# A two-layer decoder in float32: layer-1 self-attention in two steps a unit instead of three, with other PSUM banks, copies and context transposes

## The chip, the cores and the metric

The kernel runs on one core of a Trainium2 chip. TensorE (PE) multiplies and transposes, VectorE (DVE), ScalarE (ACT) and GpSimd (POOL) do the rest, and SyncE (SP) and POOL issue DMAs. PE writes to PSUM[...]. The metric is the device time of one execution in microseconds, the median of several.

## The reference, cut to what matters

A batch of 8 sequences of 512 tokens, width 256, in float32, goes through two layers. The normalisation is without weights.

```python
x = layernorm(x + L0_attn(x))            # 16 heads of 16, scores times a decay
x = layernorm(x + L0_xattn(x, ctx, ctx)) # 64 context tokens, masked
x = layernorm(x + L0_ffn(x))             # butterfly transforms
x = layernorm(x + L1_attn(x))            # below
x = layernorm(x + L1_xattn(x, ctx))      # below
x = layernorm(x + L1_ffn(x))             # 8 experts, the best 2 for each token

# L1_attn: 16 heads of 64, rotary positions, causal
q, latent = x @ wq.T, x @ w_kv_down.T
k, v = latent @ w_k_up.T, latent @ w_v_up.T
q, k = q * cos + rotate_half(q) * sin, k * cos + rotate_half(k) * sin
attn = softmax(q @ k.T / 8 + causal);  out = (attn @ v) @ wo.T

# L1_xattn: 8 heads of 64; keys and values of x (512) and of ctx (64) side by side
k, v = concat(x @ Wk1, ctx @ Wk2), concat(x @ Wv1, ctx @ Wv2)
out = softmax(x @ Wq1 @ k.T / 8) @ v @ Wo + bo
```

## The kernel before, in words

All eight sequences stay in SBUF. The stages follow one another: layer-0 self-attention (with the butterfly matrices built on POOL beside it), layer-0 context attention and feed-forward, layer-1 self-attention, layer-1 context attention with the routing of tokens, experts. The program is written as a sequence of operations. A list scheduler gives each engine its order from costs and dependencies, except where `manual_schedule(engines={PE})` keeps PE in the order of the program: that holds for the context stage of layer 1, not for its self-attention. `_pipeline` (L32) runs units through stages with offsets, and after each step it takes one piece from a list of put-off work (`put_off`: halves of the output projection).

PSUM is split into three pools: `s_tile` for scores (two banks a tile), `t_tile` for transposes and `o_tile` for sums. In layer 1 they hold 2, 2 and 2 tiles. `evac` (L98) copies PSUM to SBUF, in turn on DVE (L102) and ACT (L104).

**Layer-0 self-attention.** A unit is a sequence and four heads; `l0_project` (three units ahead) makes q and k and copies them with ACT (L404, L405). `l0_maxima` (L419, L424) makes scores for the row maxima, `l0_probs` (L468 to L477) the transposed probabilities, `l0_values` (L488) the sums. `later` holds the previous sequence's projection and the next one's preparation; `normed` then runs on ACT (L215).

**Layer-1 self-attention.** A unit is a pair of heads (b, c), with 8 units in a sequence and 64 in all. `l1_prepare` gives `share` once a sequence (x transposed, latent), `q_and_k` (s_q L844 and L845; the rope multiplies L849 and L850 on DVE; then four DMAs L853 from POOL that add the half turned by 32 rows into qk) and `v` (t_v L860, copied by ACT L862). `l1_pre` takes these from `ahead`. Rows of scores go in the groups (0, 1), (2,), (3,), that is 128 and 256, 384, and 512 columns; each group is a step. The stages of a step are, one behind the other: `l1_scores` (L899, then `masked_softmax`: L265 adds the mask and reduces on DVE, L275 scales the maximum, L277 is ACT's exp; then `scaled`: L883, L885 on DVE), `nothing`, `l1_transposes` (L931, copies by `evac`), `l1_values` (L955). The output projection `o_out` is L233.

**Layer-1 context attention.** A unit is a sequence and a pair of heads, with four row blocks (steps). `l1x_pre` makes q, k and v (L1020, L1027), and once a sequence the context values (o_v2, in the profile o_v L1008, 64 rows); `l1x_scores` 512 and 64 columns for each head (L1047, L1048), the maximum on DVE (L1049), the exp on ACT (L1050); `l1x_transposes` the four 128-column blocks of each head (L287); `l1x_last_transposes` the last 64 columns (L1069, one for each head, into half of the partitions); `l1x_values` the sums (L1081, and L1088 for the context).

Zero fills of a scratch area for the routing (64 DMAs from SP) run at the start of layer 1.

Of the kernel before, what the change touches and what calls it, by code (L numbers as in the profile page):

```python
# [49 lines left out]
def decoder_kernel(ctx: ExitStack, tc: tile.TileContext, a: dict, out: bass.AP):  # L50
# [19 lines left out]
    @contextmanager  # L70
    def psum(name, s, t, o):

        with (
            tc.tile_pool(name=f"ps_s{name}", bufs=s, space=PSUM) as pp["s"],
            tc.tile_pool(name=f"ps_t{name}", bufs=t, space=PSUM) as pp["t"],
            tc.tile_pool(name=f"ps_o{name}", bufs=o, space=PSUM) as pp["o"],
        ):
            yield
# [14 lines left out]
    def o_tile(name):  # L93
        return pp["o"].tile([P, 512], F32, tag="o", name=name)

# [128 lines left out]
    def project_and_norm(b, lhs, w, n, plus, later=None):  # L224
# [3 lines left out]
        def piece(i2):  # L228
            o = o_tile("o_out").rearrange("p (i n) -> p i n", i=2)
# [23 lines left out]
    def pt_tile():  # L253
        return ph.tile([P, 2, NT, P], F32, tag="pt", name="pt")
# [4 lines left out]
    def masked_softmax(s, p, m, n, scale, add_or_mult, sums, at):  # L259

        mx = col("mx", 2)
        nm = col("nm", 2)
        op, reduced = add_or_mult
        for j in range(2):
            dve.tensor_tensor_reduce(  # L265
                out=p[:, j, 0:n],
                in0=s[:, j, 0:n],
                in1=m,
                scale=1.0,
                scalar=-3.0e38,  # L270
                op0=op,
                op1=reduced,
                accum_out=mx[:, j : j + 1],
            )
        dve.tensor_scalar(nm, mx, -scale, None, ALU.mult)  # L275
        for j in range(2):
            act.activation(  # L277
                p[:, j, 0:n], p[:, j, 0:n], AF.Exp,
                bias=nm[:, j : j + 1], scale=scale, accum_out=sums[:, at + j : at + j + 1],
            )  # L280
# [262 lines left out]
    with tc.tile_pool(name="bfly", bufs=1, side="right") as bfly, phase("l0_self") as ph, psum("a", 3, 1, 1):  # L543
# [36 lines left out]
        for n, (b, g) in enumerate(units):  # L580
# [3 lines left out]
            for kt in range(NT):  # L584
# [17 lines left out]
                elif later:  # L602
                    later.pop(0)()
                for _ in range(3 - kt % 2):
                    next(butterfly, None)
            if n + 3 < len(units):
                l0_project(*units[n + 3])
# [12 lines left out]
    ctx.enter_context(psum("b", 2, 2, 2))  # L620
# [205 lines left out]

    def l1_prepare(b, c):
# [3 lines left out]
        def share():  # L831
            xT = x_transposed(b)
            latT = work.tile([P, S], F32, tag="lat", name="lat")
            o = o_tile("o_lat")
# [37 lines left out]
    def l1_pre(b, c, m):  # L872

        if (b, c, m) == (0, 0, 0):
            for _ in range(3):
                ahead.pop(0)()
        if ahead and (m or c == 7):
            ahead.pop(0)()
# [8 lines left out]
    put_off = []  # L887

    def l1_scores(b, c, m):
# [18 lines left out]
        for g, i in enumerate(GROUPS[m]):  # L908
            n = (i + 1) * P
            masked_softmax(  # L910
                s[:, :, at : at + n], p[:, :, at : at + n], causal[:, S - n : S], n, 1.0 / 8.0, (ALU.add, ALU.max), sums, 2 * g
# [12 lines left out]
    def l1_transposes(b, c, m):  # L924
        p = live.pop(("p", b, c, m))
        pt = pt_tile()
        order = [at for block in l1_blocks(m) for _, at in block]
        for j in range(2):
# [3 lines left out]
            evac(pt[:, j, 0 : len(order), :], t[:, 0 : len(order), :])  # L932
# [33 lines left out]
    with phase("l1_self") as ph:  # L966
        _pipeline(
            [(b, c, m) for b in range(NB) for c in range(8) for m in range(len(GROUPS))],
            [l1_pre, l1_scores, nothing, l1_transposes, l1_values],
            put_off,  # L970
        )
# [17 lines left out]
    for c in range(4):  # L989
        o = o_tile("o_k2")  # L990
# [10 lines left out]
    def l1x_pre(b, c, i):  # L1001
        if i:
            return
        if c == 0:
            xT = x_transposed(b)
            o = o_tile("o_v2")
            for kc in range(KC):
                pe.matmul(  # L1008
                    o[0:S2, :], lhsT=ctxT[:, kc, b * S2 : (b + 1) * S2], rhs=wv2[:, kc, :], start=(kc == 0), stop=(kc == KC - 1)
                )  # L1010
            vx = work.tile([P, S], F32, tag="lat", name="vx")
            evac(vx[0:S2, :], o[0:S2, :])
            live["xT", b], live["vx", b] = xT, vx
# [24 lines left out]
    def l1x_scores(b, c, i):  # L1038
# [4 lines left out]
        for j in range(2):  # L1043
# [12 lines left out]
    def l1x_transposes(b, c, i):  # L1056
        p = live["p", b, c, i]
        if i == 0:
            live["pt", b, c] = pts[c % 2], ph.tile([P, 2, S], F32, tag="pt2", name="pt2")
        pt, _ = live["pt", b, c]  # L1060
        probs_transposed(p, [pt[j][:, :, i * P : (i + 1) * P] for j in range(2)], NT)

    def l1x_last_transposes(b, c, i):

        p = live.pop(("p", b, c, i))
        _, pt2 = live["pt", b, c]
        t = t_tile("tP2")
        for j in range(2):
            pe.transpose(t[0:S2, j, :], p[:, j, S : S + S2], ident)  # L1069
        evac(pt2[0:S2, :, i * P : (i + 1) * P], t[0:S2, 0:2, :])  # L1070

    def l1x_values(b, c, k):
# [83 lines left out]
    def route_picks(b):  # L1156
        xnT = live.pop(("xnT", b))
        o = o_tile("o_r")[:, 0 : NT * NE].rearrange("p (i e) -> p i e", e=NE)
# [36 lines left out]
    def route_places(b):  # L1195

        picks, both = live.pop(("picks", b))
        o = o_tile("o_rank")
# [184 lines left out]
    def moe_down(n):  # L1383
# [3 lines left out]
        o = o_tile("o_y").rearrange("p (i n) -> p i n", i=TILES)  # L1387
# [162 lines left out]
```

## Time and profile before

| | |
|---|---|
| median of 3 runs | 3716.97 us (3712.23 to 3719.49) |
| profiled execution | 3704.71 us, span 3703.0 us |
| granted clock of PE, mean | 0.961 |
| busy: PE, DVE, ACT, POOL | 3483.6, 2190.3, 1447.7, 1091.5 us |
| layer-1 self-attention | from 1266 to 2226 us |
| layer-1 context attention | from 2226 to 3135 us |
| experts | from 3135 us on |

The times of lines and waits below are of the one profiled execution, which is 12.3 us under the median. A row of the page's fifth section or of the groups view names line, engine, operation, tiles, shapes and count; then the busy time in us and the mean of one in ns; then the engine's idle time just before, and what ended it. In the view of waits a row is: what waited, what it waited for, and the total in us, the number of times and the longest. In the timeline a row begins with the start and the length in us.

### The profile page before, as it was taken

How to read it: one execution, taken by the hardware profiler on the slowest of the kernel's cores; microseconds unless marked ns; L12 is line 12 of the kernel's file. 1: busy time of each engine (PE TensorE's matmuls, PEld its weight loads, DVE VectorE, ACT ScalarE, POOL GpSimd, SP SyncE). 2: the span in 40 equal slices, each digit the busy share in tenths (PEclk: the TensorE clock that was granted, in tenths of full speed). 3: DMA queues.
4: the chain of work that ended last, by engine and by line, in shares of the span. 5: the costliest groups of instructions: out<-in, count | busy, mean ns of one | idle time of the engine just before them, and what ended most of it. 6: DMA issues, size and time to landing. Idle time of an engine off the chain costs nothing. (4 is left out here: it accounts for less than half of the span.)

```text
span 3703.0 us, 53042 instructions
## 1 busy us (share of the span) xinstructions
PE 3483.6 (94%) x19862; PEld 2149.2 (58%) x19862; DVE 2190.3 (59%) x6160; ACT 1447.7 (39%) x2949; POOL 1091.5 (29%) x960
## 2 busy tenths in 40 slices
PE   8999899988999899999999999999999998999995
PEld 3344334446666556665666665555555555888884
DVE  5766777647666377778777775665666655110102
ACT  2444444443333244445444443433334333222222
POOL 3877787751211122222222210010101101222222
PEclk8999999987999999999999999999999999999997
DMA  4100011120000395233222320000000001766674
GB/s 130 30 24 24 24 37 36 35 59 9 4 1 1 84 277 120 35 41 40 37 35 35 41 41 1 6 13 18 18 11 14 18 12 58 241 188 180 185 232 136
DMA packets 165363, 233.94 MB, mean 63 GB/s; under 512 B 26441, under 2 KB 128521, under 8 KB 165106
## 3 DMA queue, kind: packets, MB, share of 16 engines
q1 hardware_dynamic: 138370, 174.78, 15.1%
q0 software_dynamic: 25584, 51.57, 9.4%
q10 hardware_dynamic: 1152, 4.19, 0.3%
q8 instruction: 157, 2.57, 0.3%
q14 instruction: 100, 0.82, 0.1%
HBM read 135.83 MB, written 61.11 MB: 53 GB/s over the span
## 5 line engine op out<-in xcount | busy, mean ns | idle before, releaser
L424 DVE CUSTOM_DVE_ANT_0 scored<-s_sc,decay 128x512 f32<-128x512 f32 x512 | 323.2, 687 | 231.1 <-PE s_sc L419 229.9
L853 POOL DMA_DIRECT2D qk<-turned x256 | 202.8, 1206 | 668.8 <-PE t_v L860 284.1
L477 ACT ACTIVATE pt<-s_st 128x1024 f32<-128x1024 f32 x256 | 261.3, 1024 | 263.0 <-PE s_st L473 232.0
L277 ACT ACTIVATE p<-p,nm 128x128 f32<-128x128 f32 (+3 forms) x512 | 283.1, 554 | 160.4 <-DVE nm L275 157.5
L104 ACT COPY pt<-tP 128x512 f32<-128x512 f32 (+2 forms) x416 | 212.5, 511 | 298.3 <-PE tP L931 196.9
L1050 ACT ACTIVATE p<-s_sc,nm 128x576 f32<-128x576 f32 x256 | 189.7, 743 | 294.6 <-DVE nm L1049 256.5
L885 DVE TENSOR_SCALAR p<-p,rsum 128x576 f32<-128x576 f32 (+4 forms) x768 | 296.2, 427 | 5.5
L1410 DVE TENSOR_SCALAR y<-o_y,share 128x256 f32<-128x256 f32 x71 | 31.4, 480 | 403.6 <-PE o_y L1390 403.6
L1373 PE MATMUL s_h<-xnT,we 128*128 128x256 f32 (+1 forms) x1248 | 262.4, 364 | 1.9 <-DMA we<-in_mo_w 1.9
L102 DVE COPY pt<-tP 128x512 f32<-128x512 f32 (+2 forms) x416 | 248.3, 597 | 14.8 <-PE tP L1069 6.8
L1390 PE MATMUL o_y<-we,h 128*128 128x256 f32 x1136 | 251.6, 379 | 0.0
L265 DVE CUSTOM_DVE_ANT_0 p<-s_sc,tabs 128x128 f32<-128x128 f32 (+3 forms) x512 | 233.0, 484 | 20.7 <-PE s_sc L899 20.7
L1373 PEld LDWEIGHTS s_h<-xnT,we 128*128 128x128 f32 x1248 | 218.1, 193 | 27.1 <-DMA we<-in_mo_w 2.3
L1390 PEld LDWEIGHTS o_y<-we,h 128*128 128x128 f32 x1136 | 215.2, 190 | 28.9
L1411 POOL DMA_INDIRECT total<-y,to x71 | 110.1, 1551 | 397.3 <-DVE y L1410 206.0
L899 PE MATMUL s_sc<-qk 64*128 64x256 f32 (+3 forms) x1024 | 207.8, 477 | 18.3 <-DMA qk<-turned 16.3
L1049 DVE TENSOR_REDUCE nm<-s_sc 128x1 f32<-128x576 f32 x256 | 183.2, 749 | 57.2 <-PE s_sc L1048 56.7
L931 PEld LDWEIGHTS tP<-ident,p 128*128 128x128 f32 x1280 | 137.6, 141 | 127.2 <-issue 59.9
L931 PE MATMUL tP<-ident,p 128*128 128x128 f32 x1280 | 193.9, 284 | 12.0 <-DVE pt L102 8.0
L419 PE MATMUL s_sc<-k,q 32*128 32x512 f32 x1024 | 174.4, 680 | 28.4 <-ACT k L405 26.1
L1216 POOL DMA_INDIRECT rows_in<-z,irow x64 | 63.0, 985 | 451.9 <-DVE hit L1211 349.6
L955 PE MATMUL o_pv<-pt,vc 128*64 128x128 f32 (+1 forms) x2304 | 185.5, 294 | 0.0
(282 smaller groups left out, 6657.1 us busy)
## 6 DMA issues: line engine op xcount, KB each, us to landing
we<-in_mo_w SPq DMA_DIRECT2D x78, 1024.0 KB, 6.1
rows_in<-zero SPq DMA_DIRECT2D x64, 530.0 KB, 11.4
qk<-turned POOLq DMA_DIRECT2D x256, 128.0 KB, 4.5
coef<-in_ff_upw SPq DMA_DIRECT2D x40, 256.0 KB, 3.3
coef<-in_ff_dnw SPq DMA_DIRECT2D x40, 256.0 KB, 3.3
xr<-rows_in SPq DMA_DIRECT2D x32, 265.0 KB, 6.3
x<-in_x SPq DMA_DIRECT2D x8, 512.0 KB, 9.7
total<-x SPq DMA_DIRECT2D x8, 512.0 KB, 2.9
```

The lines of the kernel that those rows point to most:

```text
L102: dve.tensor_copy(dst, src)
L104: act.copy(dst, src)
L265: dve.tensor_tensor_reduce(out=p[:, j, 0:n], in0=s[:, j, 0:n], in1=m, scale=1.0, scalar=-3.0e38, op0=op, op1=reduced, accum_out=mx[:, j : ...
L277: act.activation(p[:, j, 0:n], p[:, j, 0:n], AF.Exp, bias=nm[:, j : j + 1], scale=scale, accum_out=sums[:, at + j : at + j + 1],)
L424: dve.tensor_tensor_reduce(out=scored[:, h, :], in0=s[:, j, :], in1=decay[:, i, :], scale=1.0, scalar=-3.0e38, op0=ALU.mult, op1=ALU.max, ...
L477: act.activation(pt, s, AF.Exp, scale=1.0 / 16.0)
L853: pool.dma_start(out=qk[h : h + 32], in_=other[g : g + 32], accum_op=ALU.add)
L885: dve.tensor_scalar(p[:, j, 0:n], p[:, j, 0:n], rsum[:, j : j + 1], None, ALU.mult)
L899: pe.matmul(s[:, j, at : at + n], lhsT=q[h : h + 64, i * P : (i + 1) * P], rhs=k[h : h + 64, 0:n], start=True, stop=True,)
L931: pe.transpose(t[:, n, :], p[:, j, at * P : (at + 1) * P], ident)
L1373: pe.matmul(s[:, j, :], lhsT=w1[:, c, f * P : (f + 1) * P], rhs=xnT[:, c, :], start=(c == 0), stop=(c == KC - 1),)
L1390: pe.matmul(o[:, i, :], lhsT=h[:, f, i * P : (i + 1) * P], rhs=w2[:, f, :], start=(f == 0), stop=(f == 7),)
```

## The change

- In layer 0 `l0_project` of the unit three ahead stands before the piece from `later` in the last step of a unit.
- The PSUM pools are made with `reuse_waits="tile"`. From layer-1 self-attention on they hold 2 score tiles, 3 for transposes and 1 for sums; o_out, o_lat, o_v2, o_k2, o_r, o_rank and o_y take a tile for transposes (`u_tile`).
- `masked_softmax` reduces the negated, scaled scores, so that the operation L275 is gone.
- Layer-1 self-attention has two steps a unit, the row groups (0, 1) and then (2, 3). The stages `nothing` and one step of delay are gone; a step issues scores, transposes of the previous step's first group, the preparing piece, transposes of its second group, and values of the step before that. The copies of transposes are all on ACT, into three buffers. As before, PE's order in this stage comes from the list.
- In the context stage the last 64 columns of the two heads lie side by side (the second head's scores put the context first), and one full transpose takes both, ahead of the other transposes of the step. Context values are made for two sequences at once; two small DMAs turn their halves into a second copy, so that each head finds its rows in its own half of the partitions.

The lines left out exchange `o_tile` for `u_tile` only.

```diff
+        pool_of = partial(tc.tile_pool, space=PSUM, reuse_waits="tile")
         with (
-            tc.tile_pool(name=f"ps_s{name}", bufs=s, space=PSUM) as pp["s"],
-            tc.tile_pool(name=f"ps_t{name}", bufs=t, space=PSUM) as pp["t"],
-            tc.tile_pool(name=f"ps_o{name}", bufs=o, space=PSUM) as pp["o"],
+            pool_of(name=f"ps_s{name}", bufs=s) as pp["s"],
+            pool_of(name=f"ps_t{name}", bufs=t) as pp["t"],
+            pool_of(name=f"ps_o{name}", bufs=o) as pp["o"],
         ):
+            pp["one"] = o == 1
             yield
...
         return pp["o"].tile([P, 512], F32, tag="o", name=name)
+    def u_tile(name):
+        return t_tile(name).rearrange("p i n -> p (i n)") if pp["one"] else o_tile(name)
...
         def piece(i2):
-            o = o_tile("o_out").rearrange("p (i n) -> p i n", i=2)
+            o = u_tile("o_out").rearrange("p (i n) -> p i n", i=2)
             for j in range(2):
...
-    def pt_tile():
-        return ph.tile([P, 2, NT, P], F32, tag="pt", name="pt")
+    def pt_tile(bufs=2):
+        return ph.tile([P, 2, NT, P], F32, tag="pt", name="pt", bufs=bufs)
...
-    def masked_softmax(s, p, m, n, scale, add_or_mult, sums, at):
-        mx = col("mx", 2)
+    def masked_softmax(s, p, m, n, scale, sums, at):
         nm = col("nm", 2)
-        op, reduced = add_or_mult
         for j in range(2):
             dve.tensor_tensor_reduce(
...
                 in1=m,
-                scale=1.0,
-                scalar=-3.0e38,
-                op0=op,
-                op1=reduced,
-                accum_out=mx[:, j : j + 1],
+                scale=-scale,
+                scalar=3.0e38,
+                op0=ALU.add,
+                op1=ALU.min,
+                accum_out=nm[:, j : j + 1],
             )
-        dve.tensor_scalar(nm, mx, -scale, None, ALU.mult)
         for j in range(2):
...
                 p[:, j, 0:n], p[:, j, 0:n], AF.Exp,
-                bias=nm[:, j : j + 1], scale=scale, accum_out=sums[:, at + j : at + j + 1],
+                bias=nm[:, j : j + 1], scale=-1.0, accum_out=sums[:, at + j : at + j + 1],
             )
...
                             later.extend(l0_output(b - 1))
-                elif later:
-                    later.pop(0)()
+                else:
+                    if kt and n + 3 < len(units):
+                        l0_project(*units[n + 3])
+                    if later:
+                        later.pop(0)()
                 for _ in range(3 - kt % 2):
                     next(butterfly, None)
-            if n + 3 < len(units):
-                l0_project(*units[n + 3])
         l0_values(*units[-1], NT - 1)
...
-    ctx.enter_context(psum("b", 2, 2, 2))
+    banks = ExitStack()
+    banks.enter_context(psum("b", 2, 2, 2))
...
+    banks.close()
+    ctx.enter_context(psum("c", 2, 3, 1))
     def l1_prepare(b, c):
...
-    def l1_pre(b, c, m):
-        if (b, c, m) == (0, 0, 0):
-            for _ in range(3):
+    STEPS = ((0,), (1, 2))
+    def l1_pre(b, c, step):
+        for _ in range(2 if (c, step) == (6, 1) else 1):
+            if ahead:
                 ahead.pop(0)()
-        if ahead and (m or c == 7):
-            ahead.pop(0)()
...
     put_off = []
+    def groups(stage, some=slice(None)):
+        def run(b, c, step):
+            for m in STEPS[step][some]:
+                stage(b, c, m)
+        return run
...
             masked_softmax(
-                s[:, :, at : at + n], p[:, :, at : at + n], causal[:, S - n : S], n, 1.0 / 8.0, (ALU.add, ALU.max), sums, 2 * g
+                s[:, :, at : at + n], p[:, :, at : at + n], causal[:, S - n : S], n, 1.0 / 8.0, sums, 2 * g
             )
...
         p = live.pop(("p", b, c, m))
-        pt = pt_tile()
+        pt = pt_tile(bufs=3)
         order = [at for block in l1_blocks(m) for _, at in block]
...
                 pe.transpose(t[:, n, :], p[:, j, at * P : (at + 1) * P], ident)
-            evac(pt[:, j, 0 : len(order), :], t[:, 0 : len(order), :])
+            act.copy(pt[:, j, 0 : len(order), :], t[:, 0 : len(order), :])
         live["pt", b, c, m] = pt
...
     with phase("l1_self") as ph:
+        for _ in range(3):
+            ahead.pop(0)()
         _pipeline(
-            [(b, c, m) for b in range(NB) for c in range(8) for m in range(len(GROUPS))],
-            [l1_pre, l1_scores, nothing, l1_transposes, l1_values],
+            [(b, c, step) for b in range(NB) for c in range(8) for step in range(len(STEPS))],
+            [
+                (0, groups(l1_scores)),
+                (1, groups(l1_transposes, slice(0, 1))),
+                (0, l1_pre),
+                (1, groups(l1_transposes, slice(1, 2))),
+                (2, groups(l1_values)),
+            ],
             put_off,
...
             xT = x_transposed(b)
-            o = o_tile("o_v2")
-            for kc in range(KC):
-                pe.matmul(
-                    o[0:S2, :], lhsT=ctxT[:, kc, b * S2 : (b + 1) * S2], rhs=wv2[:, kc, :], start=(kc == 0), stop=(kc == KC - 1)
-                )
-            vx = work.tile([P, S], F32, tag="lat", name="vx")
-            evac(vx[0:S2, :], o[0:S2, :])
-            live["xT", b], live["vx", b] = xT, vx
+            if b % 2 == 0:
+                o = u_tile("o_v2")
+                for kc in range(KC):
+                    pe.matmul(
+                        o, lhsT=ctxT[:, kc, b * S2 : (b + 2) * S2], rhs=wv2[:, kc, :], start=(kc == 0), stop=(kc == KC - 1)
+                    )
+                vx = [ph.tile([P, S], F32, tag=f"vx{n}", name="vx") for n in range(2)]
+                evac(vx[0], o)
+                for n in range(2):
+                    sp.dma_start(out=vx[1][S2 * n : S2 * (n + 1)], in_=vx[0][S2 * (1 - n) : S2 * (2 - n)])
+                live["vx", b], live["vx", b + 1] = vx, vx[::-1]
+            live["xT", b] = xT
         xT = live["xT", b]
...
             s = s_tile("s_sc").rearrange("p t n -> p (t n)")
-            pe.matmul(s[:, 0:S], lhsT=lhsT, rhs=k[h : h + 64, :], start=True, stop=True)
-            pe.matmul(s[:, S : S + S2], lhsT=lhsT, rhs=k2[h : h + 64, c, b * S2 : (b + 1) * S2], start=True, stop=True)
-            dve.tensor_reduce(nm[:, j : j + 1], s[:, 0 : S + S2], AX.X, ALU.max, negate=True)
-            act.activation(
-                p[:, j, :], s[:, 0 : S + S2], AF.Exp, bias=nm[:, j : j + 1], accum_out=sums[:, j : j + 1]
-            )
+            pe.matmul(s[:, S * j : S * (j + 1)], lhsT=lhsT, rhs=k[h : h + 64, :], start=True, stop=True)
+            at = S - S2 * j
+            pe.matmul(s[:, at : at + S2], lhsT=lhsT, rhs=k2[h : h + 64, c, b * S2 : (b + 1) * S2], start=True, stop=True)
+            s = s[:, at * j : at * j + S + S2]
+            dve.tensor_reduce(nm[:, j : j + 1], s, AX.X, ALU.max, negate=True)
+            act.activation(p[:, j, :], s, AF.Exp, bias=nm[:, j : j + 1], accum_out=sums[:, j : j + 1])
         scaled(p, sums, S + S2)
...
     def l1x_transposes(b, c, i):
-        p = live["p", b, c, i]
+        p = live.pop(("p", b, c, i)).rearrange("p j n -> p (j n)")
         if i == 0:
-            live["pt", b, c] = pts[c % 2], ph.tile([P, 2, S], F32, tag="pt2", name="pt2")
-        pt, _ = live["pt", b, c]
-        probs_transposed(p, [pt[j][:, :, i * P : (i + 1) * P] for j in range(2)], NT)
-    def l1x_last_transposes(b, c, i):
-        p = live.pop(("p", b, c, i))
-        _, pt2 = live["pt", b, c]
-        t = t_tile("tP2")
+            live["pt", b, c] = pts[c % 2], ph.tile([P, S], F32, tag="pt2", name="pt2")
+        pt, pt2 = live["pt", b, c]
+        t = t_tile("tP2")[:, 0, :]
+        pe.transpose(t, p[:, S : S + P], ident)
+        evac(pt2[:, i * P : (i + 1) * P], t)
         for j in range(2):
-            pe.transpose(t[0:S2, j, :], p[:, j, S : S + S2], ident)
-        evac(pt2[0:S2, :, i * P : (i + 1) * P], t[0:S2, 0:2, :])
+            t = t_tile("tP")
+            for k in range(NT):
+                pe.transpose(t[:, k, :], p[:, (S + P) * j + k * P : (S + P) * j + (k + 1) * P], ident)
+            evac(pt[j][:, :, i * P : (i + 1) * P], t)
...
             h = c * P + 64 * j
-            pe.matmul(o[64 * j : 64 * (j + 1)], lhsT=vx[0:S2, h : h + 64], rhs=pt2[0:S2, j, :], start=False, stop=True)
+            pe.matmul(o[64 * j : 64 * (j + 1)], lhsT=vx[j][64 * j : 64 * (j + 1), h : h + 64], rhs=pt2[64 * j : 64 * (j + 1), :], start=False, stop=True)
...
             [(b, c, i) for b in range(NB) for c in range(4) for i in range(NT)],
-            [(0, l1x_pre), (1, l1x_scores), (3, l1x_transposes), (7, l1x_values), (3, l1x_last_transposes)],
+            [(0, l1x_pre), (1, l1x_scores), (3, l1x_transposes), (7, l1x_values)],
             put_off,
```

More of the change, by code (lines that the diff above doesn't have):

```diff
@@ L833, in share @@
             latT = work.tile([P, S], F32, tag="lat", name="lat")
-            o = o_tile("o_lat")
+            o = u_tile("o_lat")
             for k in range(KC):
@@ L989, in decoder_kernel @@
     for c in range(4):
-        o = o_tile("o_k2")
+        o = u_tile("o_k2")
         for kc in range(KC):
@@ L1157, in route_picks @@
         xnT = live.pop(("xnT", b))
-        o = o_tile("o_r")[:, 0 : NT * NE].rearrange("p (i e) -> p i e", e=NE)
+        o = u_tile("o_r")[:, 0 : NT * NE].rearrange("p (i e) -> p i e", e=NE)
         for i in range(NT):
@@ L1197, in route_places @@
         picks, both = live.pop(("picks", b))
-        o = o_tile("o_rank")
+        o = u_tile("o_rank")
         for i in range(NT):
@@ L1386, in moe_down @@
         xr, _, w2, cells = live.pop(("load", n))
-        o = o_tile("o_y").rearrange("p (i n) -> p i n", i=TILES)
+        o = u_tile("o_y").rearrange("p (i n) -> p i n", i=TILES)
         for i in range(size):
```

## The prediction

> **What bounds the kernel now.** I read the page's first section, then the waits of PE, then the stretches, then one unit of layer 1 instruction by instruction.
>
> ```profile
> PE 3483.6 (94%) x19862; PEld 2149.2 (58%) x19862; DVE 2190.3 (59%) x6160; ACT 1447.7 (39%) x2949; POOL 1091.5 (29%) x960
> ```
> ```profile
> PE s_sc L419 <- ACT k L405: 26.1, 7, 4.8
> PE tP L1069 <- ACT pt L104: 17.6, 50, 1.5
> ...
> PE s_sc L899 <- DMA qk<-turned: 16.3, 6, 7.0
> PE tP L1069 <- DVE pt L102: 10.5, 11, 2.4
> ```
> PE is the bound (no other engine is over 59%), and its named waits are few: 26 us in layer 0, 28 us at the small transposes of the context attention (L1069), 16 us for the rope DMAs, all at the start of layer 1. By stretch: layer-1 self-attention 1266 to 2226 (PE 929 busy of 960), context 2226 to 3135 (852 of 909), experts from 3135 (520 of 568).
>
> A unit (two heads) of layer-1 self-attention, as PE's timeline has it (start, length, line):
> ```profile
> 1799.38 1.98 PE L844 MATMUL s_q<-xT,wqT 128*128 128x512 f32 x4
> 1801.20 1.02 PE L845 MATMUL s_q<-lat,kd_ku 128*128 128x512 f32 x2
> 1802.15 0.93 PE L899 MATMUL s_sc<-qk 64*128 64x128 f32 x8
> 1803.01 0.88 PE L931 MATMUL tP<-ident,p 128*128 128x128 f32 x6
> 1803.81 0.87 PE L955 MATMUL o_pv<-pt,vc 128*64 128x256 f32 x8
> 1804.61 1.16 PE L860 MATMUL t_v<-vu,lat 128*128 128x128 f32 x8
> 1805.70 0.92 PE L899 MATMUL s_sc<-qk 64*128 64x384 f32 x4
> 1806.55 1.43 PE L931 MATMUL tP<-ident,p 128*128 128x128 f32 x8
> ...
> 1811.60 0.70 PE L844 MATMUL s_q<-xT,wqT 128*128 128x512 f32 x1
> ```
> A unit is 1811.60 − 1799.38 = 12.22 us without idle time. The x8 row of transposes takes 1.36 us to the next start; at the 0.136 a transpose of the two x6 rows (0.80 / 6) it would be 1.09, so 0.27 us is a bank wait inside a "busy" row.
>
> The rope chain sets what may follow: s_q, two multiplies on DVE, four DMAs from POOL, and only then scores.
> ```profile
> DMA to landing us min/median/max: 3.1/4.5/13.4
> ```
> (answer for tile qk.) Over all 64 units the trace gives: `turned` ends 3.39 us after s_q; the four DMAs land 3.6, 5.1, 6.1 and 7.0 us after that; the next unit's first score starts 12.15 us after s_q. So 1.7 us are spare. While the 64 zero fills run (1266 to 1403, the 13.4 above) the second landing is at 8.6.
>
> [...] the 0.27 us above counts as busy, so I count start to start. [...]
>
> **The change, part by part.**
>
> *1. Layer 0: l0_project goes ahead of the piece from `later`.* At 349.29 PE waits 4.45 us: ACT had 4 normalising activations (L215, 2.07 us together) queued ahead of the q and k copies (L404, L405), and those waited for DVE and POOL statistics. With the copies first, k is ready about 4 us sooner, but the second score tile still needs a bank whose users stand behind the same activations, so of 26.1/7 = 3.7 us an event I take back about 1.1: 7 × 1.1 = 8. The piece's own matmuls now come some 3 us later, pushing the normalised x; I charge 5. **−3 us** (−10 to +3).
>
> *2. masked_softmax: the scaling folds into the reduction.* 256 nm operations (L275, 256 × 168 ns = 43.1 us on DVE) go. DVE is busy 79% of steady layer-1 self-attention (712.7 of 905, 1300 to 2205), under PE's 883: this lies beside PE. **0**, but the exponent comes 0.17 us sooner. It can't cost anything: no instruction is added.
>
> *3. Copies of transposes all on ACT.* 128 × 548 + 64 × 675 ns = 113.4 us leave DVE (`pt` L102); ACT gets 128 × 470 + 64 × 568 = 96.5, and goes from 437 to 534 of 905. Covered by PE. What queues behind them on ACT are the exps and the vc copy, 0.5 us each. **0** (0 to +6), counted in the chain below.
>
> *4. Two steps a unit, PE's order left to the list; banks 2/3/1.* The built order of most units becomes Q (s_q, 2.77 us), scores 128 of one head and 256, 8 transposes, values, scores 384 and 512, 6 transposes, t_v, values, scores 128 of the other head, 6 transposes. I take the durations of the old unit and drop the bubble and one change of kind: 2.77 + .84 + 1.02 + .80 + 1.71 + .80 + 1.09 + 1.63 + .41 + .80 = 11.87, i.e. −0.35 a unit. Against this stands the rope. The first score that needs a unit's Q now stands 2.77 + .41 + .80 ahead of the end of the next unit's Q, so PE reaches it 11.87 − 3.98 = 7.9 us after its own Q, where before it had 12.15. In these units DVE also has a reciprocal ahead of `turned` that waits for ACT's exp; I put `turned` at +3.8. Its head needs the second landing: 3.8 + 5.1 = 8.9. So PE stands 1.0: the unit is 8.9 + 3.98 = 12.9, **+0.7** on 12.22. A second chain (scores 512 wait for the bank until `turned` has read s_q at +3.85; the last transposes wait for scale 256 at +4.95) gives 12.9 as well.
>
> The order differs within a batch of 8: three such units; two with no score between Q and transposes, where `turned` comes at +2.4 (that is what the trace has when it follows qk directly) and the head at 2.4 + 5.1 = 7.5, so 7.5 + 3.98 = 11.5; two with a 7.0 us half of o_out (20.1 and 18.5, against 18.8 and 20.06); one with x's transposes and latents, 17.0 against 16.04. Sum 2 × 11.5 + 20.1 + 18.5 + 3 × 12.9 + 17.0 = 117.3 a batch, against 116.1 to 116.4 now: +1.1, times 8 = +9. The first batches lie under the fills: second landing 8.6, so 3.8 + 8.6 + 3.98 = 16.4 against some 15.5 now, over about 9 units: +8. No DMA is added here; POOL has only these (203 us busy of 960). **+17 us** (−20 if every landing is early enough, +60 below).
>
> *5. Context: one full transpose for the two heads' last 64 columns, ahead of the others, three banks.* 256 small transposes (L1069, .34 us to the next start for a pair) go, 128 full ones of .11 come: −.23 a step. Steps with other PE work (o_v's 64-row part, 24 times; a piece of projection, about 48) are PE's: 72 × .24 = 17. The 53 plain steps (median 3.95 between scores) have another limit: scores → reduce .75 twice → exp, the bank back 2.4 to 2.85 after; with scores' 1.22 that is 3.65 to 4.1. I take .1 each: 5. Context values for two batches at once: 8 runs of 2.34 us (L1008) become 4 of 1.8: 18.7 − 7.2 = 11.5. Eight SP DMAs of 128 KB at most are new; they are read 7 steps (27 us) later, against 4.5 us for a DMA like it, so 0; SP's queue has nothing urgent there. If DVE binds, none of the 17 is got. **−33 us** (−60, if L1069's 28 us all return, to −12).
>
> *6. Experts, context routing:* o_y, o_r, o_rank take their bank from the three. Their PE order stays, and the copy out of the single o bank (.7 us) is over 1 us earlier than the bank's next use. **0** (±4).
>
> Sum: −3 + 17 − 33 = −19 us. The profiled execution (span 3703.0, its time 3704.7) is 12.3 below the median of 3716.97, so: profile about 3686, **median about 3698**.
>
> **Rivals.**
> - *Slower: the rope decides everywhere.* One mechanism: four DMAs issued in turn from POOL, read 4 us sooner than before. My 8.9 rests on the second landing at 5.1; if the scores wait for the fourth (7.0), or if `turned` slips behind DVE's reductions by 2 us, a unit is 3.8 + 7.0 + 3.98 = 14.8, +2.6, in the 24 plain units and, at half that, the 40 others with their cover: 62 + 50 = 112 in all, less if only the plain ones: 62. I take 80 in place of 17: median 3698 + 63 = 3761. It decides against the change from +36 in this stage, that is plain units over about 13.4. For it: the 1.7 us spare are all spent, and the 16.3 us wait exists already. Against: in the old order 58 of 64 units never waited.
> - *PE gets its 0.35 everywhere*, since `turned` comes no later than +2.4 with DVE 157 us lighter: −20 instead of +17, median 3661. For: DVE's 113 + 43 us. Against: the second landing still is at 7.5 with 7.9 needed, no margin.
> - *The context stage is held by DVE and the score banks.* DVE's share of a plain step is 3.4 of 3.95. Then only 12 of the 33 come: about 3719, no change.
> - *The three banks don't free anything* (0.27 and L1069's waits reappear at the single o bank, between one unit's last values and its copy): +.5 × 64 units, to 3730.
>
> "No change" is within 0.2% (7.4 us), about what a measurement of this kernel can tell.
>
> **Chances.** Forecast 0.38 (its own range 3680 to 3712); PE gets all 0.16; context held 0.13; banks 0.05; rope 0.28. Faster: nearly all of the first (.36) and the second (.16): 0.52. Same: .02 + most of the third (.10): 0.12. Slower: the rest, 0.36. The range takes the forecast, context and banks whole, two thirds of "PE gets all" and the lower half of the rope case: 3655 to 3760.
>
> **What would show it.** Right: plain layer-1 units of 12.5 to 13.2 us with the s_sc line waiting on DMA qk<-turned in tens of places; `pt` copies on ACT alone; L1008 in 4 runs; no wait at the small transposes; plain context steps 3.7 to 3.9. Wrong: units at 11.9 without DMA waits, or over 13.4; context stage not shorter than 890; s_sc<-ACT k in layer 0 still 26 us.

## The result, and the profile after

The changed kernel takes 3738.13 us (median of 6 runs, 3728.50 to 3751.08), the kernel before, timed beside it, 3713.59 (6 runs). The ratio is 1.0073, with an interval of 1.0047 to 1.0099: slower by some 27 us, where the prediction had 19 less. Differences of measured times are worked out from the ratios here and below. The two profiled executions lie further apart than the medians, 3745.3 against 3703.0 us of span: that of before is among its fastest, that of after among its slowest, and the trace of after has 344 us of halved PE clock in it against 294. So the stages below tell where the time goes, and sums are taken from the timed runs.

The page's first section, and the waits of PE (what waited, for what; total us, times, longest):

```profile
PE 3471.3 (93%) x19718; PEld 2182.6 (58%) x19718; DVE 2075.5 (55%) x5710; ACT 1507.7 (40%) x3139; POOL 1093.8 (29%) x960
```
```profile
PE s_sc L917 <- DMA qk<-turned: 50.1, 22, 10.7
PE s_sc L917 <- DVE turned L859: 25.3, 51, 1.9
PE s_sc L423 <- ACT pt L481: 23.2, 6, 3.9
...
PE s_sc L423 <- ACT k L409: 0.2, 1, 0.2
```
PE works 12 us less and the program is longer: PE waits. The rope DMAs hold it for 50 us (16 before), and a wait that hardly existed, scores behind `turned` (the rope's second multiply, which reads the score tile of s_q), comes 51 times. In layer 0 the wait for k is gone and one for `pt` stands in its place. The small transposes of the context stage are no longer in the list.

Stages, from the trace (first s_q, first matmul of o_k and last o_pv as borders), in us:

| stage | before | after | difference | predicted |
|---|---|---|---|---|
| layer 0, to the first s_q | 1267.5 | 1267.2 | −0.3 | −3 |
| layer-1 self-attention | 958.2 | 1017.2 | +59.0 | +17 |
| layer-1 context | 899.6 | 877.1 | −22.5 | −33 |
| experts to the end | 577.7 | 583.8 | +6.1 | 0 |

Self-attention unit by unit, start of s_q to start of s_q. The first eleven units (0 to 10), most of them under the zero fills, take 194.8 us against 170.3. From then on a sequence repeats; units 40 to 47:

| unit | before | after | prediction |
|---|---|---|---|
| 40 (no score after Q) | 11.89 | 11.58 | 11.5 |
| 41, 42 (with a half of o_out each) | 18.90, 20.24 | 19.70, 19.07 | 20.1, 18.5 |
| 43 (no score after Q, after the halves) | 12.18 | **14.46** | **11.5** |
| 44, 45, 46 (plain) | 12.22, 12.22, 12.21 | 12.72, 12.72, 13.27 | 12.9 each |
| 47 (transposes of x, latent) | 16.04 | 17.10 | 17.0 |
| sum | 115.9 | 120.6 | 117.3 |

All but one are within 0.6 us. Unit 43, from the timeline of after on PE and DVE (start, length, line; in brackets the idle time before and what ended it):

```profile
1950.32 1.02 PE L854 MATMUL s_q<-lat,kd_ku 128*128 128x512 f32 x2
...
1952.55 0.17 DVE L892 RECIPROCAL rsum<-sums 128x2 f32<-128x2 f32 x1 [0.30 <-ACT p L281]
1952.75 0.62 DVE L894 TENSOR_SCALAR p<-p,rsum 128x256 f32<-128x256 f32 x2
...
1953.28 1.22 DVE L858 TENSOR_TENSOR qk<-s_q,tabs 128x1024 f32<-128x1024 f32 x1
1954.41 1.22 DVE L859 TENSOR_TENSOR turned<-s_q,tabs 128x1024 f32<-128x1024 f32 x1
...
1955.78 2.06 PE L917 MATMUL s_sc<-qk 64*128 64x512 f32 x4 [1.91 <-DVE turned L859]
...
1957.77 1.54 PE L949 MATMUL tP<-ident,p 128*128 128x128 f32 x6
```
s_q ends at 1951.34. The rope's two multiplies stand on DVE behind a reciprocal that waits for ACT's exp, and behind the scaling, and begin only at 1953.28; `turned` ends 4.29 us after s_q. Until then s_q holds one of the two score tiles, and the 512-wide scores wait 1.91 us for it. Then they take 1.99 us to the next start where they take 1.06 in the next unit, and the transposes 1.33 where they take 0.71. Two stretches of that unit say why (us; length, busy of PE, PEld, DVE, ACT, POOL; then PE's granted clock, DMA share, GB/s):

```profile
1952.42:1955.83 3.41, 1.50 (x14) 0.67 (x10) 3.25 (x6) 1.42 (x5) 0.00 (x0) 1.00 0.00 0
1955.83:1959.24 3.41, 3.41 (x11) 1.91 (x12) 2.12 (x10) 1.78 (x5) 3.08 (x4) 0.50 0.53 56
```
After the wait PE's clock is halved (0.50 granted) for 3.41 us. The clock record of this trace has 50 halved stretches, all whole multiples of 3.41 us but the last, at the program's end. Here a wait of 1.91 us was followed by such a stretch of 3.41. So this wait costs twice.

In the trace of before s_q of unit 43 ends at 1905.96, and DVE goes on with

```profile
1905.96 0.17 DVE L883 RECIPROCAL rsum<-sums 128x2 f32<-128x2 f32 x1 [0.99 <-ACT p L277]
...
1907.31 0.87 DVE L885 TENSOR_SCALAR p<-p,rsum 128x512 f32<-128x512 f32 x2
1908.09 1.22 DVE L850 TENSOR_TENSOR turned<-s_q,tabs 128x1024 f32<-128x1024 f32 x1
```
Here too a reciprocal that waits for ACT and a scaling stand among the rope's multiplies, and `turned` ends 3.35 us after s_q. The longer pipeline hides it: the unit takes 12.18 us.

### The profile page after: what moved, and what is told of

Its sections match the earlier page's. It is cut to its first block, busy times and chain, and to the rows that moved or that the text cites. A ratio compares the mean times of both kernels' runs of the same rounds, so it can differ in the third digit from the quotient of the medians.

```text
span 3745.3 us, 52820 instructions
## 1 busy us (share of the span) xinstructions
PE 3471.3 (93%) x19718; PEld 2182.6 (58%) x19718; DVE 2075.5 (55%) x5710; ACT 1507.7 (40%) x3139; POOL 1093.8 (29%) x960
## 3 DMA queue, kind: packets, MB, share of 16 engines
q1 hardware_dynamic: 139010, 175.83, 15.5%
## 4 chain that ended last, share of the span: by engine, by line
PE 52%; DVE 11%; DMA 6%; ACT 5%; issue 2%; POOL 1%; POOLq 0%; DVEq 0%; SPq 0%; ACTq 0%
PE s_h L1403 6%; PE o_y L1420 6%; PE o_out L239 4%; PE s_sc L1079 4%; PE s_h L752 3%; DMA qk<-turned 3%; PE s_q L853 3%; PE s_qk L1051 3%; PE o_out L775 3%; PE o_pv L1111 2%; PE tP L949 2%; PE tP L1099 2%; PE s_sc L917 2%; ACT p L281 2%; DMA rows_in<-z,irow 2%
## 5 line engine op out<-in xcount | busy, mean ns | idle before, releaser
L917 PE MATMUL s_sc<-qk 64*128 64x128 f32 (+3 forms) x1024 | 216.0, 479 | 87.5 <-DMA qk<-turned 50.1
L270 DVE CUSTOM_DVE_ANT_0 p<-s_sc,tabs 128x128 f32<-128x128 f32 (+3 forms) x512 | 225.5, 482 | 48.3 <-PE s_sc L917 48.1
L950 ACT COPY pt<-tP 128x384 f32<-128x384 f32 (+1 forms) x384 | 181.3, 506 | 162.7 <-PE tP L949 161.6
L1403 PEld LDWEIGHTS s_h<-xnT,we 128*128 128x128 f32 x1248 | 218.4, 193 | 26.1 <-DMA we<-in_mo_w 1.3
L1079 PE MATMUL s_sc<-k,q 64*128 64x512 f32 x512 | 197.8, 654 | 13.5 <-ACT p L1084 7.2
L423 PE MATMUL s_sc<-k,q 32*128 32x512 f32 x1024 | 175.5, 675 | 25.8 <-ACT pt L481 23.2
L917 PEld LDWEIGHTS s_sc<-qk 64*128 64x128 f32 x1024 | 90.7, 188 | 181.1 <-issue 88.3
## 6 DMA issues: line engine op xcount, KB each, us to landing
rows_in<-zero SPq DMA_DIRECT2D x64, 530.0 KB, 13.4
```

Source lines behind the costliest of these rows:

```text
L270: dve.tensor_tensor_reduce(out=p[:, j, 0:n], in0=s[:, j, 0:n], in1=m, scale=-scale, scalar=3.0e38, op0=ALU.add, op1=ALU.min, accum_out=nm[ ...
L917: pe.matmul(s[:, j, at : at + n], lhsT=q[h : h + 64, i * P : (i + 1) * P], rhs=k[h : h + 64, 0:n], start=True, stop=True,)
L1079: pe.matmul(s[:, S * j : S * (j + 1)], lhsT=lhsT, rhs=k[h : h + 64, :], start=True, stop=True)
L1403: pe.matmul(s[:, j, :], lhsT=w1[:, c, f * P : (f + 1) * P], rhs=xnT[:, c, :], start=(c == 0), stop=(c == KC - 1),)
```

## Experiments

All ratios are to the kernel before, timed beside each run on the same chip.

**1. The context part alone.**

```diff
+    banks.close()                               # behind l1_self
+    ctx.enter_context(psum("c", 2, 3, 1))
...
-            [(0, l1x_pre), (1, l1x_scores), (3, l1x_transposes), (7, l1x_values), (3, l1x_last_transposes)],
+            [(0, l1x_pre), (1, l1x_scores), (3, l1x_transposes), (7, l1x_values)],
```

The functions named there, and `u_tile`, are those of the change.

> The kernel before with the context part of the change alone: one full transpose for both heads' last columns, context values for two sequences at once, banks 2/3/1 from the context stage on. Theory (the loss of the change sits in layer-1 self-attention alone, and the stages add up): the context stage, 900 us from the first o_k matmul to the last context sum before and 877 in the changed kernel, is 877 here too, self-attention stays at 958, and the time falls by 18 to 26 us (ratio 0.993 to 0.995). Rival (the context gain is a gift of the other parts, for example of the lighter DVE or of the other clock): context stays at 890 or more, ratio 0.998 to 1.002.

Measured: 3680.88 us, ratio 0.9908 (0.9892 to 0.9924), 34 us less. The profiled stage is 873.4 (899.6 before), self-attention 960.2. The theory's place is right, and the gain in time is larger than the 18 to 26 us that were expected from one pair of traces. The old context stage takes 899.6, 908.0 and 905.2 us in the three traces that have it, the new one with three banks 864.8 to 877.1, 871.4 on average, in ten: 33 us less. The prediction's −33 was right.

**2. The same with two banks.**

```diff
-    ctx.enter_context(psum("c", 2, 3, 1))
+    ctx.enter_context(psum("c", 2, 2, 2))
```

> As the context part alone, but with the banks 2/2/2 of before. Theory (the gain is instructions saved on PE, the third bank only takes the wait away): the context values (11 us) and the small transposes remain a gain, but three transposes tiles a step in two banks wait for their copies again, as before at the small ones: half of the gain, 8 to 14 us. Rival (banks decide nothing, PE's instructions everything): the same 18 to 26 us as with three. Second rival (the wait is what counted): no gain, 0 to 5 us.

Measured: 3794.61 us, ratio 1.0196 (1.0172 to 1.0219). None of the three had this: the context stage takes 992.9 us, 120 more than with three banks. Waits of PE:

```profile
PE tP L1083 <- ACT pt L110: 82.4, 64, 3.2
PE tP L1083 <- DVE pt L108: 59.3, 53, 2.4
```
The single transposes of both heads' ends now come first in a step, so three transpose tiles follow one another on PE. With two banks the third waits for the copy of the first, 142 us in all. By groups in this stage, the kernel before and the context part with three banks:

```profile
L1069 PE MATMUL tP<-ident,p 128*64 128x128 f32 x256 | 53.6, 292 | 29.2 <-ACT pt L104 17.6 <-DVE pt L102 10.5
L1008 PE MATMUL o_v<-v_o,ctxT 128*64 128x512 f32 x32 | 20.9, 789 | 0.0
```
```profile
L1078 PE MATMUL tP<-ident,p 128*128 128x128 f32 x128 | 42.7, 334 | 0.0
L1020 PE MATMUL o_v<-v_o,ctxT 128*128 128x512 f32 x16 | 10.8, 810 | 0.0
```
Half of the instructions, and no idle time ahead of them (the last column; 29.2 before). The instructions saved gain nothing while two banks make PE wait: the third bank is the condition of the gain. What it would be worth with the old transposes was not tried.

**3. The self-attention part alone.**

From the changed kernel, with the functions of the context stage and the loop of layer 0 put back:

```diff
+    banks.close()                               # behind l1_self
+    ctx.enter_context(psum("d", 2, 2, 2))
...
-            [(0, l1x_pre), (1, l1x_scores), (3, l1x_transposes), (7, l1x_values)],
+            [(0, l1x_pre), (1, l1x_scores), (3, l1x_transposes), (7, l1x_values), (3, l1x_last_transposes)],
```

> The kernel before with the self-attention part of the change alone (two steps a unit, fused scaling, copies on ACT, banks 2/3/1 in this stage); layer 0 and context are those of before. Theory: self-attention takes 1010 to 1020 us from the first s_q to the first o_k (958 before), the time rises by 40 to 60 us, ratio 1.011 to 1.016. Rival (much of the profiled loss is a slow clock of that one execution): the stage is under 995 and the ratio 1.005 to 1.009.

Measured: 3779.46 us, ratio 1.0174 (1.0158 to 1.0190), 65 us more; the stage takes 1011.1. The theory's place is right, its size a little low. In this profile the rest of the program is 11 us slower too (context 908.0 for 899.6), which is within what the same context stage varies by between traces (run 4: 905.2).

**4. Layer 0 alone.**

The kernel before with the exchange of `l0_project` and the piece from `later`, and nothing else.

> The kernel before with the exchange in layer 0 alone. Theory (one wait in the place of another: s_sc L419 behind ACT's k copies goes, and the same ACT is waited for at the pt copies instead): layer-0 self-attention ends within 5 us of before (o_bias at 826), the time within 0.2%. My forecast of -3 us can't be told from it. Rival (the wait was a net loss): 10 us or more are gained, ratio under 0.9975.

Measured: 3707.44 us, ratio 0.9976 (0.9967 to 0.9986), 9 us less. Between theory and rival. PE's longest wait in layer 0 is then:

```profile
PE s_sc L419 <- ACT pt L477: 23.2, 6, 3.9
```
One wait in the place of another, 23.2 us for 26.1, as the theory says; yet the swap is worth more than that difference. The clock accounts for it in size: the mean granted clock of these runs is 0.9599, of the 25 of before 0.9566, and among those 25 the time falls by about 2.7 us for each 0.001 of clock, 9 us for this difference. That the exchange itself brings the higher clock is not shown.

The runs of 1, 3 and 4 add up: −34 + 65 − 9 = +22, measured +27 (17 to 37).

**5. s_q half a unit earlier.**

```diff
-        for _ in range(3): ahead.pop(0)()
+        for _ in range(4): ahead.pop(0)()
-            qk = ph.tile(..., bufs=2)
+            qk = ph.tile(..., bufs=3)
```

> The changed kernel with one more piece taken from `ahead` at the start (four for three) and three qk buffers for two, so that s_q of a unit stands half a unit (6 us) earlier. Theory (the rope chain is what the two-step pipeline waits for: 50 us at the DMAs, 25 us behind `turned`): plain units fall from 12.72 to 11.8 to 12.1 us, the units after the projections from 14.46 to about 12.2, the stage from 1017 to 960 to 980, ratio to the kernel before 0.985 to 0.995. Rival (the two score tiles are the limit: s_q holds one until `turned` has read it, wherever it stands): the wait moves from the DMA to `turned`, stage 1005 or more, ratio 1.004 to 1.008.

Measured: 3654.24 us, ratio 0.9839 (0.9811 to 0.9867). The stage takes 933.2, 84 less than in the changed kernel; plain units 11.98 to 12.10, unit 43 11.77. PE no longer waits for `turned` at all, and the wait for the DMAs stands at its size of before (16.3):

```profile
PE s_sc L917 <- DMA qk<-turned: 16.4, 7, 7.5
```
Two lines undo the whole loss, and more than the 960 to 980 that were expected for the stage. What the two-step pipeline lacked is lead between s_q and what needs it. The third buffer goes with the lead and was not tried apart; the list also moved both halves of o_out into one unit (26.35 us), so the stage compares better than single units do.

**6. The zero fills in layer 0.**

```diff
-    for n in range(64): sp.dma_start(out=fills[n], in_=zero...)      # ahead of layer 1
+                if kt % 2: sp.dma_start(out=fills[2 * n + kt // 2], in_=zero...)   # l0_probs loop
```

> The changed kernel with the 64 zero fills issued in layer-0 self-attention, one in every second step, where DMA is 12% busy, from a zero tile of that stage. Theory (under the fills the first eight units take 16 to 19 us because the rope landings double, about 24 us more than the kernel before loses there and some 45 in all): the stage falls from 1017 to 970 to 985, layer-0 self-attention gains nothing and loses up to 5, ratio to the kernel before 0.996 to 1.000. Rival (the first units are slow because the pipeline fills and PE's clock is halved after the stage before, not by the landings): stage at 1005 or more.

Measured: 3719.75 us, ratio 1.0013 (1.0001 to 1.0024). Self-attention falls by 38 us to 978.9, and units 2 to 6 take 12.5 to 12.8 in place of 16.2 to 18.1: the first units were slow by the landings (in the changed kernel 7.7 us from issue in the median under the fills, 4.0 from 1435 us on). But layer 0 takes 850.1 us to the end of o_bias (831.9). The fills depend on nothing and were all issued from 34.6 to 169.1 us, and POOL, which builds the butterfly matrices, waits 31.5 us for its coefficients (coef), which it does nowhere in the changed kernel. That this wait makes up the 18 us is likely, not shown.

**7. Three steps again, all else as changed.**

```diff
-            [(b, c, step) ...], [(0, groups(l1_scores)), (1, groups(l1_transposes, slice(0, 1))), (0, l1_pre), ...]
+            [(b, c, m) ...], [l1_pre, l1_scores, nothing, l1_transposes, l1_values]
```

> The changed kernel with the pipeline of before in layer-1 self-attention (three steps a unit, one step between scores and transposes); fused scaling, copies on ACT, banks 2/3/1, layer 0 and context as changed. Theory (the loss is the pipeline alone): the stage returns to 950 to 965 us, the time to that of the context part less the layer-0 gain, ratio to the kernel before 0.985 to 0.991. Rival (copies on ACT behind the exps, or one bank for sums, carry a good part of the loss): stage 980 or more, ratio 0.994 or more.

Measured: 3653.81 us, ratio 0.9840 (0.9812 to 0.9868). The stage takes 933.1: not the 958 of before but 25 less, a plain unit 11.89. So the pipeline alone costs 84 us, and something else in this part gains 25 that it covers. The time is level with that of run 5: two steps with enough lead gain nothing over three.

**8. Without the rope's DMAs.**

```diff
-            for h in range(0, P, 32):
-                pool.dma_start(out=qk[h : h + 32], in_=other[g : g + 32], accum_op=ALU.add)
```

> The changed kernel without the four DMAs that add the turned half: q and k are left without the sine part of the rotation; all else is computed, and the list may place scores closer to s_q. Theory (landings decide): with no landing to wait for, plain units are 11.7 to 12.0 us and the stage is 945 to 960, fills or not. Rival (the DVE chain qk, `turned` and the score tile it holds decides, the landings only show it): plain units still over 12.4, the wait on `turned` grows over 50 us, stage 985 or more.

Measured: 3619.90 us, ratio 0.9736 (0.9712 to 0.9760). The stage takes 895.9 and a plain unit 11.43, below both expectations: the list also changed the order here. The unit after the projections, however, still takes 14.88 us, with the same instructions as the plain one behind it. PE's timeline of the two, one after the other:

```profile
1873.09 1.13 PE L914 MATMUL s_sc<-qk 64*128 64x512 f32 x4 [1.91 <-DVE turned L859]
1874.15 1.23 PE L946 MATMUL tP<-ident,p 128*128 128x128 f32 x6
1875.17 1.92 PE L866 MATMUL t_v<-vu,lat 128*128 128x128 f32 x8
1877.01 2.18 PE L970 MATMUL o_pv<-pt,vc 128*64 128x128 f32 x28
1879.12 0.93 PE L914 MATMUL s_sc<-qk 64*128 64x128 f32 x8
...
1886.12 1.13 PE L914 MATMUL s_sc<-qk 64*128 64x512 f32 x4 [0.16 <-DVE turned L859]
1887.18 0.87 PE L946 MATMUL tP<-ident,p 128*128 128x128 f32 x6
1887.89 1.06 PE L866 MATMUL t_v<-vu,lat 128*128 128x128 f32 x8
1888.87 1.75 PE L970 MATMUL o_pv<-pt,vc 128*64 128x128 f32 x28
1890.55 0.93 PE L914 MATMUL s_sc<-qk 64*128 64x128 f32 x8
```
The wait is 1.75 us longer, and the three rows behind the scores take 1.02 + 1.84 + 2.11 = 4.97 us to the next start in place of 0.71 + 0.98 + 1.68 = 3.37: the halved clock adds 1.60. Together 3.35 of the 3.45, and no DMA is in it. In unit 59 the same wait of 1.91 us is followed by no halved clock, and the unit takes 13.28 us: 1.60 less again. So the loss of this unit is one of the score tile. That of the plain units is one of landings by these runs, though the list's other order has a share in 11.43 that was not taken apart.

**9 and 10. What gains the 25 us: three steps with two banks, and three steps with the copies in turn on DVE and ACT.**

```diff
 (three steps) 9:
-    psum("c", 2, 3, 1) ahead of l1_self
+    psum("c", 2, 3, 1) behind l1_self, 2/2/2 in it
 (three steps) 10:
-            act.copy(pt[...], t[...])
+            evac(pt[...], t[...])
```

> The three-step kernel (changed in all else) with banks 2/2/2 in layer-1 self-attention; 2/3/1 only from the context stage on. In the three-step kernel a plain unit takes 11.89 us and the stage 933, against 12.22 and 958 in the kernel before. Theory (the third bank takes away the 0.27 us bubble between the two blocks of transposes): with two banks the unit is back at 12.1 to 12.25 and the stage at 948 to 960, some 17 us more than with three. Rival (the gain comes from the copies on ACT or the fused scaling, which bring the copies earlier): the unit stays at 11.85 to 12.0, the stage under 942.

> The three-step kernel with the copies of transposes in turn on DVE and ACT as before, banks 2/3/1. Theory (banks alone): unit 11.85 to 12.0, stage 930 to 940, no change against the three-step kernel. Rival (copies on ACT are what frees the banks in time): unit 12.1 or more, stage 948 or more. Both this run and the one with two banks slower would say that either alone is not enough.

Measured: with two banks 3671.63 us, ratio 0.9890 (0.9861 to 0.9918), stage 950.5, plain unit 12.14; with copies in turn 3650.90, ratio 0.9843 (0.9825 to 0.9860), stage 930.9, unit 11.89. Both are as the theories had it. The third bank is worth 17 us, the place of the copies, with three banks, nothing. The other 8 (958.2 to 950.5) come with the fused scaling, the third `pt` buffer or the copies while there are two banks; which was not tried. `reuse_waits` is not the cause: run 1 has it, and its stage takes 960.2.

**11 and 12. The fills at the start of the layer-0 feed-forward stage**, in the kernel of 5 and in that of 7:

```diff
+        zero = turned[:, 0, 0, 0:ROW]          # not in use yet
+        for n in range(64): sp.dma_start(out=fills[n], in_=zero...)
-        sp.dma_start(out=mi, ...)
+        act.dma_start(out=mi, ...)
```

> The two-step kernel with s_q half a unit earlier, and the zero fills issued at the start of the layer-0 context and feed-forward stage, where DMA is 1 to 2% busy, from columns of the still unused tile `turned`; the mask loads go through ACT's queue. Theory (under the fills units 2 to 9 wait 20 to 25 us in all for landings): self-attention falls from 933 to 905 to 915, the layer-0 stage stays at 435 to 442, ratio to the kernel before 0.976 to 0.980. Rival (what reads or writes memory there, masks and context, waits for the fills as the coefficients did in layer-0 self-attention): that stage grows by 15 or more and the ratio stays at 0.982 to 0.985.

> The same move of the fills in the three-step kernel. Theory: the same 18 to 25 us, stage 908 to 915, ratio 0.976 to 0.980, level with the two-step one. Rival: as there.

Measured: 3645.72 us, ratio 0.9828 (0.9813 to 0.9844), and 3636.04, ratio 0.9798 (0.9783 to 0.9812). Self-attention falls by 21 and 22 us to 912.6 and 911.4, as expected; the layer-0 context and feed-forward stage grows by 8 (to 443.9 and 442.7), more than the theory allowed and less than the rival's 15. In time the second is as expected. The first is not: its ratio is that of the rival, 4 us under the kernel of 5, and their intervals overlap, so a gain there is not shown. The last one is the fastest of all: three steps, third bank, fused scaling, copies on ACT, the layer-0 exchange, the context part, and fills where DMA has room (a DMA share of 0.01 in that stage in the trace of before).

## Why the prediction was wrong, point by point

- **Layer 0, −3.** Right in sign, low in size: −9. The wait for k gave way to one for `pt`, as argued, and that difference (26.1 to 23.2) is the forecast's 3. The rest came with a higher granted clock, which the working had nowhere.
- **Fused scaling and copies on ACT, 0.** The copies: right. The scaling is one candidate for 8 us that weren't foreseen.
- **Two steps, +17: the step that failed.** The stage lost 59. What was worked out for a plain unit held: `turned` at +3.70 (assumed 3.8), second landing 5.0 to 5.2 after it in most (5.1), unit 12.72 (12.9). Two terms were wrong.
  - *"Two with no score between Q and transposes, where `turned` comes at +2.4 …, so … 11.5."* One of the two, yes (`turned` at +2.54, 11.58 us). In the other it comes at +4.29: the unit before ends with the first group of the next scores (128 and 256 columns), so DVE has their scalings, and the exp that the second one waits for, ahead of the rope. The trace of before gave a warning: in unit 43 itself `turned` comes at +3.35 (lines in the section on the result) and in units 11 and 19 at +4.17; +2.4 is what it has in units 40 and 42 alone of this sequence, and the 3.39 "over all 64 units" is a median of several forms. The three steps of before hid the later ones; two did not. After the change the unit takes 14.40 to 14.46 us in five sequences, 13.42 and 12.96 in two: 18 us over 11.5 each. About 1 us in each of the five is the halved clock (14.46 against 13.42 in unit 51, which has none).
  - *"The first batches lie under the fills: +8."* The first eleven units lost 24.6. I charged one later landing a unit. I also set 16.4, for a unit without a half of o_out, against 15.5, which is the mean of the first eleven units of before with such halves in it (170.3 / 11); units 0 to 7 take 14.6 each before and 17.3 after. The stage paid 10.3 us at its start (units 0 and 1: 33.25 us against 22.98, before any steady order), and 3 to 5 us in units 3, 5, 7 and 8, where before had its spare 1.7 us.
  - These are 18 + 17 of the 42 us that are missing. The rest is spread: for example, in unit 32 the DMAs are issued 3.46 us after `turned` in both kernels; before hides it, after pays 3.9.
- **The gain of the third bank, −0.35 a unit.** It exists: 17 us with three steps, and 0.25 us in a plain unit (12.14 to 11.89), close to the 0.27 read from the trace (0.80 / 6 is 0.133, which would make it 0.29). With two the waits cover it.
- **Context, −33.** −34 in the runs. For it I counted instructions, and took the bank as one of three reasons; without it the same edit costs 73 us.
- **Experts, 0.** +6.1 in this pair of traces. Over all fourteen traces this stage takes 577.6 to 583.9 us, and 577.6 in run 1, whose banks there are those of the change: no cost is shown.
- **The rivals.** "The rope decides everywhere" was right in kind (+80 in this stage; +59) and had 0.28; its second form, `turned` 2 us later behind DVE, is what unit 43 shows (4.29 for 2.4). Its threshold, plain units over 13.4, was set in the wrong place: the loss came at 12.7, from the other units. "Context held by DVE" and "the banks free nothing" are refuted by 1 and 9.

With 59 in place of 17 and −9 in place of −3 the prediction's own sum is −9 + 59 − 33 = +17, slower; 27 were measured, and run 3 has 65 for this part.

## What to carry to other kernels

A shorter pipeline takes away cover. For each long chain that it served (here two multiplies, four DMAs, a held PSUM tile) count the new lead in every form of step the order contains, the rare ones too, and not from a median over the forms; the spare 1.7 us of before were all there was, and half a unit more of lead was worth 84 us. When one more tile is to be written ahead of others, count the banks first. Transfers that depend on nothing were issued at once here (all 64 fills from 34.6 to 169.1 us in run 6), whatever step of the loop they were written in; give them a stage with idle DMA, not a line.

## What the runs showed of the hardware that was not expected

A PE wait of 1.91 us was followed by 3.4 us at half clock: in the run without the rope's DMAs 1.60 us more on the rows behind it, nearly as much as the wait. The length of the wait alone does not decide this. In unit 51 of the changed kernel PE waits 1.91 us too, no halved stretch follows, and the unit takes 13.42 us in place of 14.46. All changes of the clock in this trace lie on one grid of 3.41 us, to within 0.01 us, from its first to its last. The two stretches of unit 43 shown above are cells of that grid; these are three cells in a row around the wait of unit 51:

```profile
2071.89:2075.30 3.41, 2.55 (x21) 1.45 (x19) 3.00 (x10) 2.52 (x9) 0.00 (x0) 1.00 0.01 2
2075.30:2078.72 3.42, 2.37 (x16) 1.65 (x17) 3.06 (x9) 1.98 (x6) 1.99 (x4) 1.00 0.21 25
2078.72:2082.13 3.41, 2.87 (x38) 2.42 (x37) 2.48 (x8) 2.07 (x6) 1.36 (x2) 1.00 0.98 118
```
In unit 43 the whole wait falls into one cell, where PE is busy for 1.50 of 3.41 us (44%), and the next cell is halved. In unit 51 the wait, from 2074.44 to 2076.35, is cut by a border of the grid; its two cells are busy for 75 and 69%, and the clock stays. It is the same throughout the self-attention stage of this trace: of its cells at full clock, the 14 that a halved one follows have PE busy for 47% at most, the other 263 for 58% at least. Over all fourteen traces the two kinds overlap only between 42 and 55% in this stage (in that of before between 42 and 46%). So in this stage the busy share of a cell told whether a halved one followed, with the border between 47 and 58% in this trace; what sets it is not shown. A wait of 1.91 us came with a unit of 14.46 us or one of 13.42, by where the grid fell.
